# Order of convolution outputs and states, one gate step, second-level weight sums, and the last quarters of the output

## The chip, the cores and the metric

The kernel runs on one core of a Trainium2 chip. The time is device microseconds (us) of one execution. The kernel before took 983.03 us, the median of three runs (983.00 to 983.55). Its engines are named as in the profile: PE (matrix multiplications, with PEld for its weight loads), DVE (vector), ACT (scalar, activation functions, and copies here), POOL (GpSimd) and SP (which here issues DMAs).

## The reference

Each of 64 heads is convolved along the sequence with its own long filter, the result is masked by a length, and a mixture of 64 experts of rank 16 follows, with the input added at the end. Without the imports and the inputs:

```python
def cond(u, length, log_dt, C, log_A_real, A_imag, D):     # u: 64 x 64 heads x 1024
    mask = arange(1024) < length[:, None]
    u_m = u * mask[:, None, :]
    A = -exp(log_A_real) + 1j * A_imag                     # 64 heads x 64 modes
    dtA = A * exp(log_dt)[:, None]
    Cs = (C[..., 0] + 1j * C[..., 1]) * (exp(dtA) - 1) / A
    K = 2 * einsum('hn,hnl->hl', Cs, exp(dtA[:, :, None] * arange(1024))).real
    y = irfft(rfft(u_m, 2048) * rfft(K, 2048))[..., :1024] # causal convolution
    return (y + u_m * D[:, None]) * mask[:, None, :]

def ffn(x, A, B, Wr):                                      # 4096 tokens x 1024
    scores = x @ Wr.T                                      # 64 experts
    top_vals, top_idx = top_k(scores, 16)
    G = scatter(softmax(top_vals), top_idx)                # 4096 x 64, zero elsewhere
    h = einsum('nd,krd->nkr', x, A)                        # rank 16 per expert
    return 2 * einsum('nkr,kdr->nd', h * G[:, :, None], B)

out = x + ffn(cond(x, ...), A, B, Wr)
```

Everything is in fp32. Since every expert's rank-16 part is computed and scaled by its gate, the two einsums of the ffn are two dense products of 1024 by 1024 weights with the tokens.

## The kernel before, in words

**Stages.** The 64 heads are worked off in 8 groups of 8 heads; a group g gives 512 tokens. A stage of the first phase computes the convolution of group g+1 while the first dense layer of group g runs between its parts. Then a second phase computes the second dense layer for all tokens.

**Convolution** (`conv`, L595). A group has four pairs of heads, i = 0 to 3. `into_states(i)` (L606) multiplies the inputs with `bt` into state contributions `pu` (L618: weights of 128 rows and 64 columns; four matmuls, which the profile holds as eight records, since an fp32 matmul leaves two), and two ACT copies (L623) bring them to `s`. `recur` (L626) runs the states through the chunks of the sequence with chains of DVE operations (`s<-s,turn`). `out_of(i)` (L665) has two halves: `inside` (L644) multiplies the inputs with the Toeplitz blocks `toep` (128 by 128 weights, two matmuls, four records) into two banks `pc`, and `across` (L653) adds the states through `w` (64 rows, 128 columns, four matmuls, eight records) to the same banks. Then a masked DVE multiplication writes `y` (L661). This text calls the matmuls of L618 *pu*, those of L644 *toep* and those of L653 *sw*. `conv` is a generator: at each `yield` one product of the first layer is run.

**First layer** (`first`, L788, and `seven`, L543). The 1024 x 1024 product is split into quarters and computed with seven products in place of eight (Strassen's scheme in Winograd's form). Each product is eight matmuls, 16 records, with 128 by 128 weights into a bank `h` (L553). DVE, ACT and POOL combine them; `finish` (L796) multiplies with the gates `gx` (L803, mostly on POOL) and stores the result to DRAM.

**Gates** (`gates`, L715; `spread_gates`, L761). Scores `psh` (L721), their transposes `psc` (L730), then a long chain on DVE (the 16 largest of each token, exponentials, division) that ends with `ex` (L755, the buffer `sa`). `spread_gates` transposes `ex` into the bank `pg` (L765), ACT copies it to `gt` (L767), sends it to DRAM, and eight loads on POOL's queue (L776) read it back spread over partitions as `gx`. The main loop says how many first-layer products come between `gates` and `spread_gates` (L1126). In the same stretch ACT works on the coefficient tables of a later group: sines, `b<-w` operations (L320), a table load (L249).

**Second phase** (`second`, L882). For each of four pairs of groups, seven second-level products are computed, n = 1, 6, 7, 2, 5, 4, 3 in this order, 28 in all, q = 0 to 27. Each again consists of seven sub-products `s` (L1033, 8 records each; sub-products 2 and 3 add to the banks of 1 and 5). DVE and POOL combine the banks with the residual input `o`. The weights of product n are factors made from the weight quarters by four additions (`second_level`, L859, output `e` in the profile). They are made when `second_level_of` is stepped, one addition per `ahead_step`, five steps per q. For n = 4 this is done in q = 0 and for n = 3 in q = 2; they are used from q = 5 and q = 6 on. In the last q, `last_out` (L987) computes sub-product 3 in two halves into the same bank as sub-product 5, and each half is added to `o` (L355) and stored as it comes.

**Order.** A tile scheduler places the instructions of each engine by data dependences and by the order of the program; some are pinned to program order. Banks of the matrix accumulator come from small pools: `ps_k` (tag `pk`: pu, psh, psc, pg and the tables), `ps_c` (`pc`), `ps_f` (`h` and most `s`), `ps`. A matmul that needs a bank waits until its last reader is done.

Of the kernel before, what the change touches and what calls it, by code (L numbers as in the profile page):

```python
# [37 lines left out]
F32 = mybir.dt.float32  # L38
# [6 lines left out]
P = 128  # L45
# [10 lines left out]
NG = NH // HG  # L56
# [4 lines left out]
HT = TOK // NS2  # L61
# [31 lines left out]
def body(ctx: ExitStack, tc, x, xo, lens, par, dvec, at, bm, wt, cst, out):  # L93
# [48 lines left out]
    def load_x(h):  # L142
        t = xp.tile([P, 2, NBLK * NB], F32, tag="x", name=f"x_{h}")
        nc.sync.dma_start(t, x[h : h + 2].rearrange("h p c -> p h c"))
        x_tiles[h] = t
# [265 lines left out]
    s, q = parts  # L411
# [183 lines left out]
    def conv(g, steps, out):  # L595
# [10 lines left out]
        def into_states(i):  # L606
            h = g * HG + 2 * i
            if h not in x_tiles:
                load_x(h)
            xt = x_tiles.pop(h)  # L610
            if g == 0 and i == GP - 1:
                s = s_more[:, : 2 * NCH * NB].rearrange("p (c k b) -> p c k b", c=2, b=NB)
            else:
                s = sp.tile([P, 2, NCH, NB], F32, tag="s", name=f"s_{g}_{i}")
            for c in range(2):
                pu = ps_k.tile([P, NCH * NB], F32, tag="pk", name=f"pu_{g}_{i}_{c}")
                for hh in range(2):
                    nc.tensor.matmul(  # L618
                        pu[hh * NS : (hh + 1) * NS, :],
                        lhsT=bt[:, i, (1 - c) * P + hh * NS : (1 - c) * P + (hh + 1) * NS],  # L620
                        rhs=xt[:, hh, : NCH * NB], start=True, stop=True,
                    )
                marks["s"] = nc.scalar.copy(s[:, c], pu.rearrange("p (k b) -> p k b", b=NB))  # L623
            states[i] = xt, s
# [40 lines left out]
        def out_of(i):  # L665
            across(*inside(i))

        def step(n):
            for _ in range(n):
                next(steps, None)  # L670
# [26 lines left out]
        yield  # L697
        step(4)
        yield 2
        into_states(2)  # L700
        out_of(0)
        yield
        into_states(3)
        recur(2, 3)
        out_of(1)
        yield
        step(5)
        yield
# [154 lines left out]
    def queued(o, i):  # L863
        tc.keep_in_program_order(nc.sync.dma_start(o, i))
# [17 lines left out]
    def second(places, rooms, loaded, next_loaded, made, second_level_of, spare, pools):  # L882
# [3 lines left out]
        op, ps, A, B = pools  # L886
        todo = [(sg, n) for sg in range(NG // 2) for n in (1, 6, 7, 2, 5, 4, 3)]
        outs, loads = {}, [0]
# [17 lines left out]
        def add(engine, o, a, b, plus):  # L906
            engine(o, a, b, ALU.add if plus > 0 else ALU.subtract)
# [5 lines left out]
        def bank_into(o, place, bank, sign):  # L913
            add(tt, o, o, bank, sign * SIGN[place])
# [9 lines left out]
        def parts_of(sg, n):  # L924
# [59 lines left out]
            early, late = into(out_(m, s), 1)  # L984
            return all_of(out_(0, 1), A, ALU.add) if n == 3 else nothing, early, stored(m, s, late)

        def last_out(product, bank):  # L987

            sg, o = NG // 2 - 1, outs[0, 1, 0, 1]
            for ii in range(2):  # L990
                product(3, bank, rows=(ii,))
                bank_into(o[:, ii], (0, 1), bank[:, ii], 1)
                (queued, scalar_queued)[ii](
                    out[2 * sg + 1, 0, 1, 0][:, ii * HT : (ii + 1) * HT], o[:, ii])

# [11 lines left out]
        for q, (sg, n) in enumerate(todo):  # L1007
            if q + 1 < len(todo):
                steps = second_sums(r_of.pop(q + 1), *rooms(q + 1))
            else:  # L1010
                steps = iter(())

            def ahead_step():
                next(later, None)
                try:
                    next(steps)
                except StopIteration as e:
                    if e.value is not None:
                        sums[q + 1] = e.value

            right_ = sums.pop(q)
            left_ = made[n]
            early, late = now
            later = second_level_of({0: 4, 2: 3}[q]) if q in (0, 2) else iter(())

            def product(i, bank=None, more=False, rows=(0, 1)):
                first = bank is None
                if first:
                    banks, t = (ps, "ps") if more else (ps_f, "pf")
                    bank = banks.tile([P, 2, HT], F32, tag=t, name=f"s{sg}_{n}_{i}")  # L1030
                for ii in rows:
                    for k in range(2):
                        nc.tensor.matmul(  # L1033
                            bank[:, ii, :], lhsT=left_[i - 1][:, k, ii * P : (ii + 1) * P],
                            rhs=right_[i - 1][:, k, :],
                            start=(first and ii == 0 and k == 0),
                            stop=(ii == 1 and k == 1 and not more),
                            skip_group_check=True,
                        )
                return bank  # L1040

            def new(t, i):
                return fp.tile([P, 2, HT], F32, tag=t, name=f"{t}{i}_{sg}_{n}")

            c11 = product(1, more=True)
            p1 = new("p", 1)
            nc.scalar.copy(p1, c11)  # L1047
            p6 = product(6)
            v2 = new("u2", 2)
            tt(v2, p1, p6, ALU.subtract)  # L1050
            early((0, 1), v2)
            ahead_step()
            p7 = product(7)
            v3 = new("u3", 3)
            tt(v3, p7, v2, ALU.add)
            early((1, 1), v3)
            early((1, 0), v3)
            if q == 0:
                sum_factors()
            product(2, c11)  # L1060
            late((0, 0), c11, None)
            ahead_step()
            c12 = product(5, more=True)
            late((1, 1), c12, v3)
            ahead_step()
            p4 = product(4)
            late((1, 0), p4, v3)
            ahead_step()
            if q + 1 < len(todo):
                product(3, c12)  # L1070
                late((0, 1), c12, v2)
            else:
                last_out(product, c12)
            ahead_step()
            if q + 1 < len(todo):
                ahead, *now = parts_of(*todo[q + 1])
                ahead()
            if n in behind:
                residuals(sg, *behind[n])
            elif n == 4 and sg + 1 < NG // 2:  # L1080
                residuals(sg + 1, 0, 0)
            if q + 4 < len(todo):
                r_of[q + 4] = places(q + 4)
                load_factor(*todo[q + 4], r_of[q + 4])
# [4 lines left out]
    def ahead(it, n):  # L1089
        for _ in range(n):  # L1090
            next(it, None)
# [12 lines left out]
    products, done = counted(first(0, y, spread)), [0]  # L1104
# [4 lines left out]
    for g in range(NG):  # L1109
        ex = gates(g, y)  # L1110
        if g:
            spread = {}
            for _ in steps:
                pass
            if g + 1 == NG:
                right.close()
                wpb = pool(ctx, "wpb", 1, "right")
                wb_quarters = quarters(wpb, bm, "wb", nc.sync)
                ahead(products, 13 - done[0])
                spread_gates(g, ex, spread)  # L1120
            for _ in products:
                pass
            products, done = counted(first(g, y, spread)), [0]
        if g + 1 == NG:
            break
        ahead(products, 1 if g == 0 else 2)  # L1126
        spread_gates(g, ex, spread)
        if g == 0:
            tables1, n = steps_of(1), 0
            while True:  # L1130
                behind_ = marks["y" if n < 6 else "ex"]
                with tc.issue_after(behind_.ins), tc.issue_after(marks["s"].ins):
                    if next(tables1, tables1) is tables1:
                        break
                if n % 3 == 2:
                    ahead(products, 1)
                n += 1
        steps = steps_of(g + 2)
        for n in conv(g + 1, steps, got):
            ahead(products, 1 if n is None else n)  # L1140
        y = got.pop()
# [5 lines left out]
    def second_level_of(n, e=None):  # L1147
        if n in made:
            return
        if e is None:  # L1150
            t = wp.tile([P, KH, L // 2], F32, tag=room_of[n], name=f"e{n}").rearrange("p k t -> p (k t)")
            e, spare[n] = part(t, 0, 3, 2, L // 4), flat(t, NE2, 2)
        made[n] = yield from second_level(wb[n - 1], e)
# [27 lines left out]
    for _ in products:  # L1181
# [3 lines left out]
        if n in (5, 6):  # L1185
            i = (1, 6)[n - 5]
# [16 lines left out]
    ps = ctx.enter_context(tc.tile_pool(name="ps", bufs=4, space=PSUM))  # L1203
# [60 lines left out]
```

## Time and profile before

| | |
|---|---|
| median of three runs | 983.03 us (983.00 to 983.55) |
| the profiled execution | 983.15 us, of it the span 981.3 us |
| clock granted to the PE | 1.0 of full speed, throughout |
| PE busy | 967.1 us (99%) |
| DVE busy | 717.5 us (73%) |
| POOL busy | 332.3 us (34%) |
| ACT busy | 159.7 us (16%) |
| first phase, steady stage (227.85 to 304.50 us) | 76.65 us |
| second phase (from 637.2 us on) | 343.8 us |

All durations in the text come from this one execution; points in time (such as "at 134 us") count from the start of its span. A row of the chain or of the timeline gives a start, a duration, the engine, the tile or the operation, the line of the kernel and a number of records. `[1.84 <-DVE sa L755]` after a row says that the engine stood for 1.84 us before it, and that what ended the wait was the DVE operation of L755 on `sa`. In the timeline the duration of a group on the PE reaches to the modelled end of its last matmul, which overlaps the start of the next group; the rows of the chain are cut at the next start.

### The profile page before, as it was taken

To read this page: it belongs to the slowest core of one execution; us is meant where nothing else is said; L and a number is where in the kernel's file an instruction comes from. 1 tells how busy PE (TensorE), PEld (TensorE's weight loads), DVE (VectorE), ACT (ScalarE), POOL (GpSimd) and SP (SyncE) were. 2 spreads that over 40 slices of the span, in tenths; PEclk is the share of its full clock that TensorE was granted. 3 is DMA by queue.
4 is the path that set the end of the run, shared out by engine and by line. 5 is a ranking of instruction groups with operands and counts; after the bars stand their busy time and mean duration, and the time that the engine had idled before them with its cause. 6 is when DMAs were issued, how large, how long until landed. Compare 5 with 4: busy or idle time off the path is not lost.

```text
span 981.3 us, 11964 instructions
## 1 busy us (share of the span) xinstructions
PE 967.1 (99%) x4312; PEld 722.8 (74%) x4312; DVE 717.5 (73%) x1681; ACT 159.7 (16%) x310; POOL 332.3 (34%) x285
## 2 busy tenths in 40 slices
PE   7999999999999999999999999999999999999998
PEld 2476656676676686586676678888888888888887
DVE  8889698587487597587566669788866785686674
ACT  5245051420231231131001000000000000000000
POOL 0212121032023022122123112246645663754565
PEclk9999999999999999999999999999999999999999
DMA  7915243325315315415405254573674466268432
GB/s 279 235 50 162 73 150 105 108 81 161 108 70 145 126 41 156 140 55 156 135 27 166 76 177 161 200 290 110 214 258 130 169 207 232 88 215 269 128 117 98
DMA packets 67457, 143.99 MB, mean 147 GB/s; under 512 B 9479, under 2 KB 18247, under 8 KB 67399
## 3 DMA queue, kind: packets, MB, share of 16 engines
q1 hardware_dynamic: 49378, 94.40, 28.8%
q0 software_dynamic: 16864, 47.22, 15.5%
q10 hardware_dynamic: 1156, 1.61, 0.6%
q8 instruction: 34, 0.56, 0.2%
q14 instruction: 25, 0.20, 0.1%
HBM read 94.89 MB, written 47.25 MB: 145 GB/s over the span
## 4 chain that ended last, share of the span: by engine, by line
PE 94%; DVE 4%; DMA 0%; issue 0%; POOL 0%; ACT 0%; DVEq 0%
PE h L553 39%; PE s L1033 34%; PE pc L644 6%; PE pu L618 5%; PE pc L653 5%; PE psh L721 3%; PE pb L326 1%; PE pk L293 1%; DVE hg L355 1%; PE pg L765 0%; PE psc L730 0%; DMA par_sb<-in_par 0%; DVE y L661 0%; DVE ty L355 0%; DVE f L366 0%
## 5 line engine op out<-in xcount | busy, mean ns | idle before, releaser
L366 DVE SCALAR_TENSOR_TENSOR s<-s,turn 128x128 f32<-128x128 f32 (+1 forms) x558 | 142.9, 303 | 34.0 <-ACT s L623 28.0
L553 PE MATMUL h<-y,waa 128*128 128x256 f32 x512 | 121.8, 384 | 0.0
L553 PE MATMUL h<-ty,was 128*128 128x256 f32 x512 | 116.9, 381 | 0.0
L553 PE MATMUL h<-y,was 128*128 128x256 f32 x512 | 116.6, 381 | 0.0
L553 PEld LDWEIGHTS h<-y,waa 128*128 128x128 f32 x512 | 93.9, 190 | 28.7 <-issue 16.8
L553 PEld LDWEIGHTS h<-ty,was 128*128 128x128 f32 x512 | 96.5, 190 | 18.1 <-issue 5.4
L553 PEld LDWEIGHTS h<-y,was 128*128 128x128 f32 x512 | 96.5, 190 | 17.9 <-issue 5.2
L803 POOL TENSOR_TENSOR hg<-h_p,gx 128x512 f32<-128x512 f32 x16 | 27.0, 1689 | 218.6 <-DVE h_p L366 215.0
L803 POOL TENSOR_TENSOR hg<-h_u,gx 128x512 f32<-128x512 f32 x32 | 47.1, 1474 | 123.0 <-DVE h_u L355 122.2
L661 DVE TENSOR_TENSOR y<-pc,mask 128x512 f32<-128x512 f32 x64 | 42.3, 684 | 35.4 <-PE pc L653 35.4
L1047 ACT COPY p<-s 128x512 f32<-128x512 f32 x28 | 16.4, 586 | 312.9 <-PE s L1033 301.5
L900 POOL TENSOR_TENSOR o<-o,acc_a 128x512 f32<-128x512 f32 x32 | 48.0, 1519 | 42.7 <-DMA r<-hg_dram 10.8
L644 PE MATMUL pc<-x,toep 128*128 128x512 f32 x128 | 61.5, 605 | 0.0
L553 PE MATMUL h<-ty,waa 128*128 128x256 f32 x256 | 58.7, 381 | 0.0
L355 DVE TENSOR_TENSOR hg<-hg 128x512 f32<-128x512 f32 x64 | 42.8, 689 | 19.0 <-POOL hg L803 18.0
L776 POOL DMA_DIRECT2D gx<-gt_dram x56 | 33.5, 630 | 66.2 <-DMA gt_dram<-gt 66.2
L553 PEld LDWEIGHTS h<-ty,waa 128*128 128x128 f32 x256 | 47.9, 190 | 10.2 <-issue 3.9
L618 PE MATMUL pu<-x,bt 128*64 128x448 f32 x256 | 55.1, 553 | 0.0
L653 PE MATMUL pc<-s,w 64*128 64x448 f32 x248 | 54.7, 561 | 0.0
L355 DVE TENSOR_TENSOR o<-o,s 128x512 f32<-128x512 f32 (+1 forms) x53 | 35.6, 672 | 25.3 <-PE s L1033 18.8
L900 POOL TENSOR_TENSOR o<-o,b_room 128x512 f32<-128x512 f32 x32 | 49.9, 1581 | 9.8 <-DVE b_room L355 9.8
L623 ACT COPY s<-pu 128x448 f32<-128x448 f32 x62 | 33.0, 532 | 119.7 <-PE pu L618 119.6
(231 smaller groups left out, 1586.5 us busy)
## 6 DMA issues: line engine op xcount, KB each, us to landing
x<-in_x SPq DMA_DIRECT2D x32, 512.0 KB
hg_dram<-hg POOLq DMA_DIRECT2D x16, 1024.0 KB, 5.5
o<-in_xo SPq DMA_DIRECT2D x64, 256.0 KB
out<-o SPq DMA_DIRECT2D x63, 256.0 KB
gx<-gt_dram POOLq DMA_DIRECT2D x56, 256.0 KB, 6.3
qy<-hg_dram SPq DMA_DIRECT2D x28, 512.0 KB
r<-hg_dram SPq DMA_DIRECT2D x26, 512.0 KB
hg_dram<-hg POOLq DMA_DIRECT2D x16, 768.0 KB, 4.3
```

The lines of the kernel that those rows point to most:

```text
L355: V.tensor_tensor(out=o, in0=a, in1=b, op=o_)
L366: V.scalar_tensor_tensor(out=o, in0=a, scalar=s, in1=b, op0=o1, op1=o2)
L553: nc.tensor.matmul(bank[:, ii, :], lhsT=fac[n - 1][:, k, (j + ii) * P : (j + ii + 1) * P], rhs=rf[n - 1][:, k, :], start=(first and ii == ...
L618: nc.tensor.matmul(pu[hh * NS : (hh + 1) * NS, :], lhsT=bt[:, i, (1 - c) * P + hh * NS : (1 - c) * P + (hh + 1) * NS], rhs=xt[:, hh, : NCH ...
L623: marks["s"] = nc.scalar.copy(s[:, c], pu.rearrange("p (k b) -> p k b", b=NB))
L644: nc.tensor.matmul(pc, lhsT=toep[:, 2 * i + hh, :], rhs=xt[:, hh, :], start=True, stop=False)
L653: m = nc.tensor.matmul(pcs[hh][:, NB:], lhsT=w[o : o + NS, c, i, 1:], rhs=s[o : o + NS, c].rearrange("p k b -> p (k b)"), start=False, sto ...
L661: marks["y"] = V.tensor_tensor(out=y[:, :, i // 2, 2 * (i % 2) + hh, :], in0=pcs[hh].rearrange("p (k b) -> p k b", b=NB), in1=mask, op=ALU ...
L776: i = queue.dma_start(gx[:, ii, :], gt_dram[g, c * n : (c + 1) * n, :].unsqueeze(1).to_broadcast([n, RANK, TOK]),)
L803: G.tensor_tensor(out=o, in0=a, in1=b, op=op)
L900: tc.keep_in_program_order(G.tensor_tensor(out=o, in0=a, in1=b, op=op_))
L1033: nc.tensor.matmul(bank[:, ii, :], lhsT=left_[i - 1][:, k, ii * P : (ii + 1) * P], rhs=right_[i - 1][:, k, :], start=(first and ii == 0 an ...
```

## The change

There are four edits.

1. In `conv` for all groups but the first, `out_of(0)` now stands before `into_states(2)`, and `out_of(1)` before `into_states(3)` and `recur(2, 3)`. Before, the states came first. Products of the first layer still stand at the `yield`s.
2. In the main loop, three instead of two first-layer products come between `gates` and `spread_gates` of group 1. The other groups keep theirs (one for group 0, two for the rest).
3. The four additions that make the factors of n = 4 are stepped in q = 1 instead of q = 0, those of n = 3 in q = 3 instead of q = 2.
4. In the last q, sub-product 5 goes into two banks, one per half (`last_but_one`), with each half added to its output as it comes and one store for both. Sub-product 3's halves add to these two banks, so the second half no longer shares a bank with the first.

As the program is built from the changed kernel, POOL and SP have the same instructions in the same order as before. ACT has the same instructions; in the stage of group 0 to 1 the copies of pair 2's states come behind eight operations of L320, a table load and the operations of L249, and in the stage of group 1 to 2 the copy of `gt` comes behind four operations of L320, and one copy of pair 1's states behind the table load.

```diff
@@ conv
         yield 2
+        out_of(0)
         into_states(2)
-        out_of(0)
-        yield
+        yield
+        out_of(1)
         into_states(3)
         recur(2, 3)
-        out_of(1)
         yield
@@ second
+        def last_but_one(product, bank):
+            o = outs[0, 1, 1, 1]
+            for ii in range(2):
+                product(5, bank[ii], more=True, rows=(ii,), first=True)
+                bank_into(o[:, ii], (1, 1), bank[ii][:, ii], 1)
+            queued(out[NG - 1, 0, 1, 1], o.rearrange("p i t -> p (i t)"))
@@ last_out
             for ii in range(2):
-                product(3, bank, rows=(ii,))
-                bank_into(o[:, ii], (0, 1), bank[:, ii], 1)
+                product(3, bank[ii], rows=(ii,))
+                bank_into(o[:, ii], (0, 1), bank[ii][:, ii], 1)
@@ loop over q
-            later = second_level_of({0: 4, 2: 3}[q]) if q in (0, 2) else iter(())
+            later = second_level_of({1: 4, 3: 3}[q]) if q in (1, 3) else iter(())
-            def product(i, bank=None, more=False, rows=(0, 1)):
-                first = bank is None
-                if first:
+            def product(i, bank=None, more=False, rows=(0, 1), first=False):
+                if bank is None:
+                    first = True
...
-                            start=(first and ii == 0 and k == 0),
-                            stop=(ii == 1 and k == 1 and not more),
+                            start=(first and ii == rows[0] and k == 0),
+                            stop=(ii == rows[-1] and k == 1 and not more),
...
-            c12 = product(5, more=True)
-            late((1, 1), c12, v3)
+            if q + 1 < len(todo):
+                c12 = product(5, more=True)
+                late((1, 1), c12, v3)
+            else:
+                c12 = [ps.tile([P, 2, HT], F32, tag="ps", name=f"last_{ii}") for ii in range(2)]
+                last_but_one(product, c12)
@@ main loop
-        ahead(products, 1 if g == 0 else 2)
+        ahead(products, (1, 3)[g] if g < 2 else 2)
```

## The prediction

> **What bounds the kernel now.** I read the page first, then the chain that ended last, then the PE's waits, then the timeline around each place that the diff touches.
>
> ```profile
> PE 967.1 (99%) x4312; PEld 722.8 (74%) x4312; DVE 717.5 (73%) x1681; ACT 159.7 (16%) x310; POOL 332.3 (34%) x285
> PE 94%; DVE 4%; DMA 0%; issue 0%; POOL 0%; ACT 0%; DVEq 0%
> ```
>
> The PE is busy for 967.1 of 981.3 us at full clock, and 94% of the chain is PE work. So time can come only from (a) PE work itself and (b) the few places where the PE stands:
>
> ```profile
> PE pg L765 <- DVE sa L755: 1.8, 1, 1.8
> PE s L1033 <- DVE acc_a L366: 1.2, 1, 1.2
> PE psh L721 <- DVE y L661: 0.9, 2, 0.6
> PE s L1033 <- DVE o L355: 0.5, 1, 0.5
> ```
>
> The first, second and fourth are at the three places that the smaller edits touch. The number of matmuls is unchanged in every edit.
>
> **Part A: out_of before into_states.** Here I compare the same group of matmuls behind different predecessors. Rows of the chain, one steady stage (start, us):
>
> ```profile
> 227.85 1.65 PE pu L618 x8
> 229.50 1.91 PE pc L644 x4
> 231.42 1.71 PE pc L653 x8
> 233.12 3.65 PE h L553 x16
> ...
> 245.91 3.46 PE h L553 x16
> 249.37 1.72 PE pc L644 x4
> 251.09 1.71 PE pc L653 x8
> 252.79 3.65 PE h L553 x16
> ```
>
> A product (h, 16 records) takes 3.46 behind another product and 3.65 behind a group with another weight shape; toep (pc L644) takes 1.72 behind a product, which has its 128x128 weights too, and 1.91 behind pu. So a change of weight shape costs 0.19. One interval of before, pu-toep-sw-h, is 1.65+1.91+1.71+3.65 = 8.92. After it is toep-sw-pu-h: 1.72+1.71+X+3.65, where X is pu behind sw (64x128 weights to 128x64). No row shows that change. X = 1.65, as behind a product, gives 8.73: 0.19 saved. Bounds for X: 1.50 if nothing is spent between two half-size shapes (the starts of single matmuls put 0.14 of the 1.65 on entering), saving 0.34; 1.84 if rows and columns changing together cost a whole 0.19 more, saving nothing. The Trainium skill (TensorEngine Tiling (Array Packing), Key Properties) says that changing the tiling mode, not just the tile, drains the engine. Taken as one price per change, before has four changes per interval and after three: the saving is again one, 0.19. Taken by the kind of change, a sw-to-pu step that alters both dimensions could be dearer; the rule states no price, so I stay with the nearest row. Two intervals in each of 7 convs: 14 x 0.19 = **2.7** (0 to 4.8).
>
> What else moves: the pu of pairs 2 and 3, their ACT copies and the DVE recurrence come some 3.5 us later in a stage. In the stage above, the copies end at 239.00 and the recurrence of pair 3 at 245.38; after, about 249. sw of pair 3 starts at 258.16: 9 us of cover; pair 2 has more. On the DVE, pair 0's y no longer sits between recurrence steps. Pair 0 must be ready one pu (1.65) earlier: its recurrence ends at 224.7 and its sw starts at 231.42, so 5 of 6.7 us remain. Nothing of SP's or POOL's queue is moved. I cost this at zero.
>
> **Part B: gates of group 1 one product later.** Around 134 us the PE has nothing to do until ex is done:
>
> ```profile
> 134.16 0.59 PE L553 MATMUL h<-y,waa 128*128 128x256 f32 x2
> 136.60 0.60 PE L765 MATMUL pg<-cst_sb,sa 128*64 128x128 f32 x4 [1.84 <-DVE sa L755]
> 137.13 0.97 PE L618 MATMUL pu<-x,bt 128*64 128x448 f32 x4
> ```
>
> With a product ahead of pg (14 more records x 0.216 = 3.0 us), pg comes at 137.8, 1.3 after ex ends at 136.45: the 1.84 is gone. But the order on ACT changes. Before, gt's copy (137.29, 0.58) is ahead of the coefficient operations of L320; after, it is behind four of them. These wait for w<-mag,sh on DVE, which waits for ACT's last sh (L267). With nothing between, sh ends near 138.2, w near 138.8 (0.69), four L320 steps of 0.29 near 140.0, gt's copy near 140.6. The second half of pu (pair 0) takes the bank that this copy frees; the PE reaches it 2.06 us after pg (138.66-136.60), at 139.8. So a **new wait of 0.8 to 1.1** arises, PE on ACT gt. Net 1.84-0.95 = **0.9** (0 to 1.84). Behind the late copy stand the first copies of s; pair 0's recurrence then ends near 150.4 and is needed at 155. The gx loads (POOL's queue) come 3 us later, near 150, against a first use near 152; that cover is thin, and if it fails POOL's products, not the PE, are late first. In group 2 the DVE's gate chain is finished 6 us before its pg.
>
> **Part C: e-sums for n=4 out of q=0 into q=1, for n=3 out of q=2 into q=3.** DVE around the stall (the PE stands from 647.43 to 648.74):
>
> ```profile
> 647.40 0.68 DVE L859 TENSOR_TENSOR e<-wba,e 128x512 f32<-128x512 f32 x1
> 648.01 0.68 DVE L366 SCALAR_TENSOR_TENSOR acc_a<-u,s 128x512 f32<-128x512 f32 x1
> 648.60 3.03 DVE L859 TENSOR_TENSOR e<-wba,e 128x512 f32<-128x512 f32 x1
> ...
> 658.36 1.41 DVE L876 TENSOR_TENSOR ey<-qy 128x512 f32<-128x512 f32 x1
> ```
>
> acc_a reads the bank that the fourth product of q=0 needs. Without the e-sums at 644.28 and 647.40 (0.60 each at the DVE's pace) it would end near 647.4: the PE's wait goes, with 0.1 of restart, **1.4**. The sums now stand in q=1, whose same read (659.69) ends at 660.37 and the PE needs the bank at 660.93: 0.5 of slack. Two sums ahead of it are 1.2, so about 0.7 late: **a new wait of 0.8** with its restart. The row of 3.03 argues that it can be more: the add normally takes 0.68, and POOL ran from 648.59 to 651.08. The Trainium skill (SBUF — State Buffer, SBUF: two separate sides) has the port pair shared by DVE and GpSimd as an exclusive lock, a two-input DVE operation waiting for the whole GpSimd operation. By the 0.60 pace q=1 costs 0.8; by that rule, with one POOL operation of 1.25 (2.49 for two, at 648.59) in the way, about 1.5. The add of 1.41 at 658.36, in q=1 itself, behaves so. I take 0.8, because the DVE has gaps of 0.9 to 1.1 before each PE result there. n=3 moves into q=3, where slack is 0.6 and only one sum stands ahead of the read: nothing, at worst 0.6. Net **0.6** (-0.7 to 1.4).
>
> **Part D: last quarters in two banks.** Tail of before:
>
> ```profile
> 975.19 1.03 PE L1033 MATMUL s<-qy,e 128*128 128x256 f32 x4
> 976.73 1.13 PE L1033 MATMUL s<-qy,e 128*128 128x256 f32 x4 [0.51 <-DVE o L355]
> 977.90 0.42 DVE L355 TENSOR_TENSOR o<-o,s 128x256 f32<-128x256 f32 x1 [1.22 <-PE s L1033]
> ```
>
> The last four records wait until DVE has read the first half of the same bank. With a bank per half they follow at 216 ns: 975.19+4x0.216 = 976.05 instead of 976.73, and 0.1 at the restart: **0.8**. Product 5 is read in halves (two adds of 0.42 for one of 0.69), about 972.8 and 973.7, while product 4 runs to 975.19: hidden. The final add and store follow 0.8 earlier.
>
> **Sum.** 2.7+0.9+0.6+0.8 = 5.0. The profiled execution took 983.15 (span 981.3 and 1.85 around it): 978.15. It lay 0.12 above the median of the runs, so on the median 978.0; I say **978.1**.
>
> **Rivals.**
> R1, stalls go and none come: A 2.7, B 1.84, C 1.4, D 0.8, sum 6.7: 976.3. For it: ACT and DVE are 16% and 73% busy. Against it: the order on ACT is fixed and puts gt behind L320.
> R2, the reorder saves nothing (X = 1.84): 5.0-2.7 = 2.3: 980.8. For it: no row shows X. Against it: every change that has a row costs 0.14 to 0.20, whatever its kind.
> R3, the second-level sums meet POOL in q=1 and q=3 and each makes a wait of 2.4 (3.03-0.60): A+B+D less 2 x 2.4 and plus 1.4 gives 1.0: 982.1, no measurable change. For it: the row of 3.03. Against it: q=1's slots before the read lie in gaps of DVE.
> R4, **slower**: the late recurrence. If the DVE reaches pair 3's steps with other sums queued first, so that s of pair 3 comes over 9 us later than today's plus my 3.5, sw stands in all 7 stages. It outweighs the 5.0 from 0.7 us a stage on; at 1.2 us a stage it costs 8.4: 986.5. For it: DVE idles 28.0 us in all on ACT's copies of s, at the head of an in-order queue, so bank-freeing sums wait behind. Against it: 9 us of cover, and the DVE is 71% busy in that stage (54.6 of 76.7).
>
> **How the numbers follow.** The case above 0.53, R1 0.18, R2 0.13, R3 0.10, R4 0.06. A measurement of this kernel can tell about 0.2% (2.0 us): faster means below 981.06, slower above 985.0. R3 and the far end of R2 are no change: 0.12; R4 slower: 0.05; faster 0.83. The likeliest case's own range is 977.0 to 979.3; with R1 below and R2 above, 976.0 to 981.2 leaves out R4, most of R3 and the far bounds of A, under 2 in 10.
>
> **What would show it.** A: sixteen-record products after pu still 3.65, toep 1.72 in all four intervals, pu behind sw near 1.65; a stage of 76.3 instead of 76.7. B: no wait of pg on sa; instead pu on ACT gt, about 1. C: no wait near 648; one near 660 of 0.5 to 0.8, none in q=3. D: no wait among the last records. I am wrong if pu behind sw takes over 1.8, if a wait of sw on s or of h on DVE appears once per stage, or if the wait in q=1 exceeds 2.

## The result and the profile after

| | before | changed |
|---|---|---|
| median of six runs each | 983.13 us (983.0 to 983.55) | 978.20 us (978.07 to 978.31) |
| ratio to before, 95% interval | | 0.9949 [0.9937, 0.9962] |
| the profiled execution, span | 981.3 us | 976.5 us |

The change gains 4.9 us, 0.5%. The prediction was 978.1. All medians of this text are of runs at 0.99 or more of the full clock; one run, of the kernel with part D undone, had 0.85 of it, took 1122.66 us and is left out.

The profile of the changed kernel, first the engines, then waits of the PE (total us, times, longest; three of the first 26 us, which the kernel before has too, are left out):

```profile
PE 963.7 (99%) x4312; PEld 723.8 (74%) x4312; DVE 724.2 (74%) x1682; ACT 159.7 (16%) x310; POOL 334.8 (34%) x285
```

```profile
PE pu L618 <- ACT gt L768: 1.2, 1, 1.2
PE pb L326 <- DVE b L366: 1.1, 2, 0.8
PE psh L722 <- DVE y L661: 0.9, 2, 0.6
PE s L1042 <- DVE acc_a L355: 0.5, 1, 0.5
PE pc L644 <- DMA toep<-krows: 0.3, 1, 0.3
```

The PE is busy for 3.4 us less with the same 4312 records. The run of part A alone, below, has 2.8 of these (964.3); the other 0.6 is not traced to a part. Three waits are gone (pg on sa, s on acc_a of 1.2, s on o) and two new ones have come (pu on gt, s on acc_a of 0.5). The waits of pb and toep lie in the first 38 us, where the tables and filters of group 0 land. By the first psh the two kernels are level all the same (51.10 before, 51.15 changed), so nothing is read from them.

The chain of the changed kernel, the same stage as in the prediction (start, us):

```profile
226.33 1.72 PE pc L644 x4
228.05 1.71 PE pc L653 x8
229.75 1.65 PE pu L618 x8
231.41 3.65 PE h L553 x16
235.06 1.72 PE pc L644 x4
```

pu behind sw takes 1.65, as it does behind a product. The interval is 1.72+1.71+1.65+3.65 = 8.73 in place of 8.92. From psh of one group to psh of the next it is 76.27 us (336.42-260.15, starts in the chain) in place of 76.67 (338.73-262.06).

The timeline of the PE at group 1's gates, then that of ACT:

```profile
133.81 3.62 PE L553 MATMUL h<-y,waa 128*128 128x256 f32 x16
137.27 0.60 PE L766 MATMUL pg<-cst_sb,sa 128*64 128x128 f32 x4
137.80 0.97 PE L618 MATMUL pu<-x,bt 128*64 128x448 f32 x4
138.70 0.70 PE L553 MATMUL h<-y,was 128*128 128x256 f32 x2
140.56 0.97 PE L618 MATMUL pu<-x,bt 128*64 128x448 f32 x4 [1.16 <-ACT gt L768]
```

```profile
138.76 0.40 ACT L320 ACTIVATE b<-w,p_alpha 128x128 f32<-128x128 f32 x1 [0.79 <-DVE w L355]
139.06 0.39 ACT L320 ACTIVATE b<-w,p_nbeta 128x128 f32<-128x128 f32 x1
139.36 0.38 ACT L320 ACTIVATE b<-w,p_alpha 128x128 f32<-128x128 f32 x1
139.65 0.39 ACT L320 ACTIVATE b<-w,p_nbeta 128x128 f32<-128x128 f32 x1
139.94 0.56 ACT L768 COPY gt<-pg 64x512 f32<-64x512 f32 x1
```

pg no longer waits. Its bank, full at 137.9, is copied only at 139.94, behind four table operations that wait for w; and the second half of pu stands for that bank.

DVE in q=1, the PE there, and the tail on the PE:

```profile
653.54 1.41 DVE L877 TENSOR_TENSOR ey<-qy 128x512 f32<-128x512 f32 x1
654.87 0.68 DVE L860 TENSOR_TENSOR e<-wba,e 128x512 f32<-128x512 f32 x1
655.47 0.68 DVE L877 TENSOR_TENSOR ey<-qy,ey 128x512 f32<-128x512 f32 x1
656.07 0.67 DVE L355 TENSOR_TENSOR acc_a<-acc_a,s 128x512 f32<-128x512 f32 x1
```

```profile
656.80 1.99 PE L1042 MATMUL s<-b_room,ey 128*128 128x256 f32 x8 [0.52 <-DVE acc_a L355]
```

```profile
967.70 1.89 PE L1042 MATMUL last<-t,e 128*128 128x256 f32 x8
969.43 1.89 PE L1042 MATMUL s<-t,wbs 128*128 128x256 f32 x8
971.15 1.89 PE L1042 MATMUL last<-qy,e 128*128 128x256 f32 x8
```

acc_a reads the bank from 656.07 on, and the PE starts at 656.80, after a wait of 0.52 (0.68 by the starts of its matmuls, with what it loses at the restart). The last eight records run through.

### The profile page after: what moved, and what is told of

Its sections match the earlier page's. It is cut to its first block, busy times and chain, and to the rows that moved or that the text cites. A ratio compares the mean times of both kernels' runs of the same rounds, so it can differ in the third digit from the quotient of the medians.

```text
span 976.5 us, 11964 instructions
## 1 busy us (share of the span) xinstructions
PE 963.7 (99%) x4312; PEld 723.8 (74%) x4312; DVE 724.2 (74%) x1682; ACT 159.7 (16%) x310; POOL 334.8 (34%) x285
## 4 chain that ended last, share of the span: by engine, by line
PE 93%; DVE 4%; DMA 1%; ACT 1%; issue 0%; POOL 0%; DVEq 0%
PE h L553 39%; PE s L1042 34%; PE pc L644 5%; PE pc L653 5%; PE pu L618 5%; PE psh L722 3%; PE pb L326 1%; PE pk L293 1%; DMA toep<-krows 1%; DMA krows<-ks 0%; PE last L1042 0%; PE pg L766 0%; DVE s L366 0%; PE psc L731 0%; DVE hg L355 0%
## 5 line engine op out<-in xcount | busy, mean ns | idle before, releaser
L366 DVE SCALAR_TENSOR_TENSOR s<-s,turn 128x128 f32<-128x128 f32 (+1 forms) x558 | 153.2, 321 | 26.5 <-ACT s L623 20.2
L355 DVE TENSOR_TENSOR o<-o,s 128x512 f32<-128x512 f32 x50 | 34.1, 682 | 23.0 <-PE s L1042 17.3
```

Source lines behind the costliest of these rows:

```text
L355: V.tensor_tensor(out=o, in0=a, in1=b, op=o_)
L366: V.scalar_tensor_tensor(out=o, in0=a, scalar=s, in1=b, op0=o1, op1=o2)
```

## The experiments

Each was measured beside the kernel before on the same chip. Unless said otherwise, a time of a whole kernel is a median of its runs.

How fine this is: the 95% interval of a ratio to before is 1.0 to 1.4 us wide to either side. Differences to the changed kernel are taken between sessions, in which the median of the kernel before lay between 983.07 and 983.57 and its fastest run between 982.85 and 983.07, so one or two tenths tell nothing. That B, C and D each gain something rests on two things: every run of the kernels with one of them undone (978.69 and more) lies above every run of the changed kernel (978.31 at most), and the wait in question comes and goes in the profiles.

**Each part by itself.** Part A alone on the kernel before, and the changed kernel with B, C or D undone.

```diff
 # part A alone, on the kernel before
+        out_of(0)
         into_states(2)
-        out_of(0)
         yield
+        out_of(1)
         into_states(3)
         recur(2, 3)
-        out_of(1)
```

> Only part A (out_of before into_states), on the kernel before. Theory of the prediction: 14 intervals save 0.19 each, 2.7 us, so 980.4, with the waits of pg on sa (1.8), of s on acc_a (1.2) and of s on o (0.5) as before. Rival (the reorder saves nothing, the gain is in the three stalls): 983.1, and then B, C and D together must be worth the whole 4.9.

Measured 980.25, ratio 0.9973 [0.9963, 0.9983], beside 983.07 before: 2.8 us. The waits of the PE in its profile, without those of the first 38 us:

```profile
PE pg L765 <- DVE sa L755: 1.8, 1, 1.8
PE s L1033 <- DVE acc_a L366: 1.2, 1, 1.2
PE psh L721 <- DVE y L661: 0.9, 2, 0.6
PE s L1033 <- DVE o L355: 0.5, 1, 0.5
```

No wait is gone and none is added, and the PE is busy for 2.8 less (964.3): the gain is PE work alone. That the reorder saves nothing is out.

```diff
 # part B undone, on the changed kernel
-        ahead(products, (1, 3)[g] if g < 2 else 2)
+        ahead(products, 1 if g == 0 else 2)
```

> The changed kernel with part B undone (two products before group 1's pg). Theory: the wait of pg on sa (1.84) comes back and the wait of pu on ACT's gt (1.2) goes, so slower by 0.6 to 0.7: 978.8 to 978.9. Rival (the new wait only moves time that is lost anyway): the same as changed, 978.2, or faster, since 1.2 of new wait would be all loss: 977.0.

Measured 978.99: B is worth 0.8. The wait of pg on sa is back with 1.8, that of pu on gt is gone.

```diff
 # part C undone, on the changed kernel
-            later = second_level_of({1: 4, 3: 3}[q]) if q in (1, 3) else iter(())
+            later = second_level_of({0: 4, 2: 3}[q]) if q in (0, 2) else iter(())
```

> The changed kernel with part C undone (e-sums in q=0 and q=2). Theory: the wait in q=0 (1.15, with its restart 1.3) comes back, the one in q=1 (0.5, with its restart 0.7) goes: slower by 0.6, 978.8. Rival (the DVE's work is late in either place, and q=1's wait stays too): slower by 1.3, 979.5.

Measured 978.73: C is worth 0.5. Its profile has the wait of 1.1 in q=0 and none in q=1.

```diff
 # part D undone, on the changed kernel
-            c12 = [ps.tile(...) for ii in range(2)]; last_but_one(product, c12)
+            c12 = product(5, more=True); late((1, 1), c12, v3)
...
-                product(3, bank[ii], rows=(ii,))
+                product(3, bank, rows=(ii,))
```

> The changed kernel with part D undone (one bank in the last quarters). Theory: the last four records wait 0.5 for DVE again, 0.7 to 0.8 with the restart: 978.9 to 979.0. Rival (the end is set by the last store, and not by the PE): 978.2, no change.

Measured 978.98: D is worth 0.8, and the wait of s on o is back with 0.5. The four are 2.82+0.79+0.53+0.78 = 4.92, against 4.93 measured for all together. They add up as well as such runs can tell, as parts should that act at four places of one chain of PE work.

**What makes the new wait behind pg.** All ACT operations of the stage are put behind the copy of gt.

```diff
+        marks["gt"] = nc.scalar.copy(gt, pg)
...
+        with tc.issue_after(marks["gt"].ins) if g == 1 else ExitStack():
             for n in conv(g + 1, steps, got):
                 ahead(products, 1 if n is None else n)
```

> The changed kernel with every ACT operation of the next stage (sines, L320, table loads, copies of s) queued behind group 1's copy of gt. Theory (ACT's order makes the wait of pu on gt): gt is copied right behind pg, near 138; the wait of 1.16 (1.3 with restart) is gone and none comes back: 976.9. Rival (ACT, now later with its tables, makes another wait in the same stage, pb on b or sw on s): 978.2 or slower.

Measured 976.69 (976.51 to 976.99), ratio to before 0.9925 [0.9913, 0.9937]. ACT and the PE there:

```profile
138.10 0.58 ACT L768 COPY gt<-pg 64x512 f32<-64x512 f32 x1 [3.64 <-PE pg L766]
```

```profile
137.41 0.60 PE L766 MATMUL pg<-cst_sb,sa 128*64 128x128 f32 x4
137.94 1.76 PE L618 MATMUL pu<-x,bt 128*64 128x448 f32 x8
```

Both halves of pu run through and no other wait has come in the stage, though the sines now end near 146.3 instead of 138.0. The order on ACT was the cause, and this kernel is faster than both: 1.5 below the changed one. All of it lies in this stage, which takes 62.57 from psh to psh in place of 64.11. That is the wait of 1.16 and, by an estimate from the prices of part A (0.19 for h behind pu, 0.14 for pu behind h), 0.33 for two changes of shape: with its bank free, pu is no longer cut in two by a pair of h records.

**What makes acc_a late in q=1.** The last of POOL's three operations on acc_a there (an addition) is left out, and with it that part of the output.

```diff
-            early((1, 0), v3)
+            if q != 1:
+                early((1, 0), v3)
```

> The changed kernel without one of POOL's three subtractions in q=1 (the last, L901 on acc_a; that part of the output is left out). The DVE's queue is unchanged. Theory (the add ey of L877 takes 1.41 instead of 0.68 because POOL is still at work): it takes 0.68, acc_a comes 0.7 earlier, the wait of s on acc_a (0.52, 0.68 with restart) is gone: 977.5. Rival (the number of sums ahead on the DVE makes the wait): ey stays at 1.4 or the wait stays at 0.5: 978.2.

Measured 977.45, 0.75 below the changed kernel. POOL ends at 653.07 now, and DVE:

```profile
653.43 0.69 DVE L877 TENSOR_TENSOR ey<-qy 128x512 f32<-128x512 f32 x1
654.04 0.68 DVE L860 TENSOR_TENSOR e<-wba,e 128x512 f32<-128x512 f32 x1
654.64 0.69 DVE L877 TENSOR_TENSOR ey<-qy,ey 128x512 f32<-128x512 f32 x1
655.24 0.68 DVE L355 TENSOR_TENSOR acc_a<-acc_a,s 128x512 f32<-128x512 f32 x1
```

The same queue, but ey takes 0.69 instead of 1.41, and the PE's wait is gone. In the changed kernel POOL's three operations end at 654.39 and ey at 654.95. The Trainium skill (SBUF — State Buffer, SBUF: two separate sides) has DVE and GpSimd share a pair of ports as an exclusive lock: a DVE operation with two inputs waits until the GpSimd operation that holds the pair is over. The rows agree, since ey ends 0.56 after POOL, about the 0.60 that one such add takes in a row of them. What is shown is that POOL's operation makes ey long; that the ports are the reason is the page's statement.

But the add of 1.41 was there before the change too, and then there was no wait, since acc_a stood right behind it. So POOL uses up most of the slack, and the two adds of 0.60 that now come in between overrun it: without POOL's last operation, or with the sums back in q=0 and q=2, the PE does not wait in q=1.

**Other places for the sums.** Three more, of which the last stands on the kernel with gt copied first.

```diff
-            later = second_level_of({1: 4, 3: 3}[q]) if q in (1, 3) else iter(())
+            later = second_level_of({2: 4, 4: 3}[q]) if q in (2, 4) else iter(())   # or (2, 3), (2, 5)
```

> The changed kernel with the e-sums for n=4 stepped in q=2 and those for n=3 in q=4. Theory: q=1's wait (0.52, 0.68 with restart) is gone, q=2 has 0.8 of slack before its read and none comes there: 977.5. Rival (every q has too little slack for two sums, and n=5's q=4 least): a wait of 0.5 to 1.5 appears in q=2 or q=4: 978 to 979.

Measured 978.90, in the rival's range but not at its places: there is no wait in q=1 to q=4, but one of 0.8 in q=5. DVE enters q=5 late with the last sum at 697.61, POOL comes late behind it, and `o` waits for POOL. In the changed kernel `o` waits for POOL just as long, but 0.8 earlier (at 704.23), where it costs the PE nothing.

```profile
703.08 0.68 DVE L355 TENSOR_TENSOR o<-o,s 128x512 f32<-128x512 f32 x1
705.04 0.69 DVE L355 TENSOR_TENSOR o<-o,s 128x512 f32<-128x512 f32 x1 [1.29 <-POOL o L901]
```

> The changed kernel with the e-sums for n=4 in q=2 and those for n=3 in q=3. Theory: the DVE runs late out of q=2 by up to four sums (2.4), and q=3's read, which has 0.2 of slack in the changed kernel, comes late: a wait of 0.5 to 1.5 in q=3 takes the place of q=1's 0.7: 977.8 to 979. Rival (the gaps of the DVE in q=2 take the sums up whole): 977.5.

Measured 978.44, with a wait of 0.4 in q=3 (0.6 by the starts of its matmuls): the theory of DVE's lateness out of q=2.

> The changed kernel with ACT's stage behind the copy of gt, as in the run on that, and the e-sums for n=4 in q=2 and for n=3 in q=5, where the DVE has no sums and no n=5. Theory: neither the wait of pu on gt (1.3) nor one in q=1 to q=5 (0.7): 978.2 - 1.3 - 0.7 = 976.2, or 975.9 from the measured 976.7 of the former. Rival (the DVE has no free place in q=5 either): a wait of 0.5 to 1.0 in q=5, 976.7 to 977.2.

Measured 977.01, above the 975.9 to 976.2 of the theory and no better than with gt first alone; the rival's time held, with a wait of 0.3 in q=5. The starts of its matmuls show 0.2 lost in q=1, where DVE puts both ey adds ahead of acc_a even without a sum, 0.45 in q=5 and 0.15 in q=6, together 0.8. By the same count the PE loses 0.7 with the sums in q=1 and q=3, 1.2 in q=2 and q=4, and 0.8 in q=2 and q=3, against 1.3 in q=0 and q=2: no place that was tried is free of loss.

**How much cover the recurrence has** (the rival that ends slower). These three stand on the kernel of the run before.

```diff
 # states last
         out_of(0)
-        into_states(2)
         yield
         out_of(1)
+        into_states(2)
         into_states(3)
         recur(2, 3)
```

> As the run before, with the states later still: out_of(0), product, out_of(1), then the states of pairs 2 and 3 and their common recurrence. By the PE's rows one change less per stage, 0.15, seven times: 975.2 if the recurrence has cover. Theory (the cover is finite: DVE needs some 10 us for the 36 operations of both pairs, its copies end near 239.3 in the stage at 226, and sw of pair 2 stands at 248.8): s is 2 us late or a little more in each of 7 stages, sw waits on DVE s, and the kernel is slower than the first: 986 to 993. Rival (the 9 us of cover hold): 975.2.

Measured 977.91: a clear miss, and in the rival's direction, though it is not faster than the run before either. There is no wait of sw on s. DVE and the PE in one stage:

```profile
238.67 8.31 DVE L366 SCALAR_TENSOR_TENSOR s<-s,turn 128x128 f32<-128x128 f32 x36 [0.94 <-ACT s L623]
```

```profile
246.82 1.88 PE L644 MATMUL pc<-x,toep 128*128 128x512 f32 x4
248.63 1.77 PE L653 MATMUL pc<-s,w 64*128 64x448 f32 x8
```

The 36 operations take 8.3 us, 0.23 each, not the 10 of the estimate, and end 1.65 us ahead of sw. The saving per stage is not there either: from psh to psh it is 76.23 (335.90-259.67) against 76.28 (334.79-258.51) in the run before, 0.05 and not 0.15, because the two pu groups in a row take 3.26 in its chain and not the 1.65+1.50 that was assumed. (The chain of the kernel before had such a row: 3.26 for the 16 pu records at 74.95.) The first of these stages is 0.8 longer than in the run before (72.87 against 72.06 from psh to psh), with one new wait there, of toep on y for 0.6; that outweighs what the others save.

> As the run before, but recur(2) stands ahead of the states of pair 3 and recur(3) behind them. Theory (only the order of the two recurrences makes pair 2 late): pair 2 is ready 3 us earlier, near 247, and pair 3, due at 256, near 250; no wait of sw on s: 975.2. Rival (DVE still interleaves the two): sw waits 0.5 to 1.5 in each of 7 stages, 979 to 986.

Its edit puts `recur(2)` between the two `into_states` and `recur(3)` behind them. Measured 977.58, with no wait of sw on s and the same wait of toep on y; that is near neither number, and it tells nothing apart, since the common recurrence was in time already.

```diff
 # states one product later
         out_of(1)
+        yield
         into_states(2)
         into_states(3)
         recur(2, 3)
-        yield
```

> As the run with the states last, and these (with the common recurrence) one more product later: out_of(0), product, out_of(1), product, states of 2 and 3, recurrence, product, out_of(2). In the run before, the recurrence of both took 8.2 us and ended 1.65 ahead of sw of pair 2; 3.65 later it ends 2.0 behind. The built order puts five matmuls of the next product (2.2 us) between toep and sw of pair 2 in the middle stages. Theory (cover ends at 1.65): sw on s waits 0 to 1 in each of 7 stages, and DVE's bank-freeing sums behind the recurrence add to it: 979 to 986. Rival (the recurrence still has cover, since products fill in): 977.5 to 978.5, no wait of sw on s.

Measured 981.81, in the range of the theory: 3.9 more than with the states last. Now the wait is there, in five of the seven stages:

```profile
PE pc L653 <- DVE s L366: 2.7, 5, 0.7
```

```profile
325.54 2.32 PE L553 MATMUL h<-ty,was 128*128 128x256 f32 x10
328.37 1.77 PE L653 MATMUL pc<-s,w 64*128 64x448 f32 x8 [0.50 <-DVE s L366]
```

The waits are 2.7 of the 3.9. Each of the seven stages also has one change of shape more (the states between two products instead of behind sw), which accounts for the rest: from psh to psh the two stages without the wait are 0.17 and 0.18 longer than with the states last, the five others 0.72 to 0.94. The scheduler had put ten records of the next product ahead of sw here (the first row), which is why the wait is 0.5 and not 2.

## Why the prediction was right

**A, 2.7: measured 2.8.** The assumed row, pu behind sw at 1.65, is what the changed kernel shows: it was the nearest row and not a reading, and it held. Going from 64x128 to 128x64 weights costs no more than going from 128x128 to 128x64. That is the reading of the Trainium skill's drain (TensorEngine Tiling (Array Packing), Key Properties) as one price per change; the dearer reading is out. No run here shows the drain itself, only its price. Its cost of zero for the later states held: pair 3's recurrence ends at 248.45 and sw starts at 256.25, 7.8 us of cover instead of 9. In the stage's own time the recurrence ended about 1 us later than worked out, since two hg adds of DVE stand between its last steps.

**B, 0.9: measured 0.8.** The mechanism, place and order were right. The gt copy ended at 140.50 (140.6 predicted). The new wait was 1.16 rather than 0.8 to 1.1, because the PE came 0.5 earlier: pg at 137.27, not 137.8. The reorder had already brought the PE forward by two intervals (0.4), which the step took from before's times. So B gave 0.8 and not 0.9. The sum missed this, as it added the parts up as if each stood alone.

**C, 0.6: measured 0.5.** The wait in q=1 is 0.52, 0.68 by the starts of matmuls, against 0.8. The step counted two sums of 0.60 ahead of acc_a. Two adds are there, but only one is an e-sum; the other is an ey add that came behind acc_a before, so the count was right by luck. Setting the meeting with POOL aside was right for another reason than the one given, DVE's gaps: the long ey was there before as well (1.41 at 658.36), so it was already in the slack of 0.5 that the step counted. q=3 has no wait, as said.

**D, 0.8: measured 0.8.** The half adds of product 5 run at 968.82 and 969.63 and are hidden.

**The sum.** It is closer than its parts: A gave 0.1 more, B and C 0.1 less each.

**The rivals.** That stalls go and none come fell with the two new waits; gt's copy first shows that it could be had for part B. That the reorder saves nothing fell with the run of A alone. That DVE and POOL make a wait of 2.4 in q=1 and q=3 fell with 0.5 and none, though POOL does lengthen an add in q=1. The late recurrence did not happen at this change. The last run shows that it does once the states of pair 2 come two products later: sw waits on s, if on pair 2 and not on pair 3.

What stays open is why no place for the two sets of sums is free of loss. The profiles name DVE's order and its meetings with POOL, in q=1 by an experiment, in q=3 and q=5 only by their rows.

## What to carry to other kernels

Where the PE is full, compare one group of matmuls behind different predecessors: a change of weight shape cost 0.14 to 0.20 us here, whatever its kind, and orders with one change less gain that much at each place. Before a wait is removed by moving work ahead of it, look at what then queues in front of the engine that frees its bank: here four small ACT operations gave back more than half of the gain, and putting the copy first on ACT won it back. Gains at separate places of one chain add up; but a shift in time from one edit belongs into the arithmetic of the next.

## What the runs showed of the hardware that was not expected

Two rows of DVE in the profile of the kernel before, the recurrence of two pairs in turn and that of one pair alone:

```profile
216.05 8.65 DVE L366 SCALAR_TENSOR_TENSOR s<-s,turn 128x128 f32<-128x128 f32 x36 [1.90 <-ACT s L623]
239.04 3.97 DVE L366 SCALAR_TENSOR_TENSOR s<-s,turn 128x128 f32<-128x128 f32 x13 [1.54 <-ACT s L623]
```

An operation takes 0.24 us with two pairs in turn (0.23 with the states last) and 0.31 with one. POOL does no arithmetic during the second row, so it is not POOL that makes it slower. In one chain most operations need the result of the one just before them, with two pairs in turn none does; that this is why they pack closer is likely, but was not tested by itself. The estimate of 10 us for 36 operations fits the pace of one chain, though the first row was there to read.
